# A two-block adaLN network on one core: k before q in the local layers, and small operations moved from GpSimd to VectorE

## The chip, the cores and the metric

The kernel runs on one core of a Trainium2 chip. The metric is the device time of one execution in microseconds (us); lower is better. Five engines work beside each other, each through its own queue in order: TensorE (PE in the profile, with its weight loads as PEld), VectorE (DVE), ScalarE (ACT), GpSimd (POOL) and SyncE (SP), which issues most of the DMAs.

## The reference

The input is x, 4 sequences of 1024 tokens with 128 features, all in float32. Two adaLN blocks follow each other. Each computes six modulation vectors from a condition c, and then

```
h = layernorm(x) * (1 + ca) + sa;  x = x + ga * attention(h)
h = layernorm(x) * (1 + cb) + sb;  x = x + gb * ffn(h)
```

Block 0 has a linear attention (softmax over features, 16 heads) and a mixture of 16 small experts. Block 1 has a causal window attention (window 64, 16 heads of 8, a global prefix of 16 tokens), and its "ffn" is two local layers. A local layer, which is where most of the change lies, is

```
h = shift_token(x)                                   # half of the features from the token before
q, k, v = split(h @ wqkv)                            # 8 heads of 64
q = q / max(|q|, 1e-12) * q_scale ; k = k / max(|k|, 1e-12) * k_scale
q, k = rotary_xpos(q, k)
o = softmax(8 * q k^T over this and the previous window of 64, masked) v
x = x + o @ wo
h = layernorm(shift_token(x)) * g + b ;  a, g = split(h @ w1 + b1) ; x = x + (a * gelu(g)) @ w2 + b2
```

The layernorm is (x - mean) / sqrt(var + 1e-5).

## The kernel before

The work is tiled by 128 tokens. Features lie on partitions (`xT`, `hT`), so that matmuls contract over them; layernorms and norms of heads are computed with tokens on partitions. The program has four stretches in time: block 0's attention (to about 75 us), the experts with the next sequences' attention woven in (to about 320 us), block 1's window attention (to about 579 us) and the local layers (to the end), 2 layers x 4 sequences x 8 tiles = 64 tiles.

PE's order is written out by hand (`manual_schedule`); the orders of DVE, ACT and POOL come from a scheduler that places each instruction by its own estimate of times. Its result for both kernels can be read from the built programs, and the prediction uses it.

`ln_in` (L133) is every layernorm's first half. DVE takes the statistics (`bn_stats`, `bn_aggr`, L144 and L146), subtracts the mean (L150); POOL adds 1e-5 to the variance (L152), raises it to the power -1/2 (L153) and multiplies (L154). `ln_out` transposes the result on PE and applies scale and bias on ACT. There are 49 such calls.

`project(l, b, t, w, ps)` (L647) makes q (w=0) or k (w=1) of one tile. PE multiplies (L653) into a bank of PSUM. ACT squares it (L656, `sq`). DVE multiplies it by the rotary cosine table (`co`, L658) and, with halves exchanged, by the sine table (`si`, L663), and sums the squares of each head (L665) into column w of `ss`, a tile of 128 x 2 x 8. POOL then, for w=1, takes the maximum of both columns with 1e-24 (L668), raises both to -1/2 (L669), adds `co` and `si` (L673, for q too), and multiplies k by its column (L675). q is not multiplied; its column enters the scores as a scale.

In the first eight tiles (`light`, layer 0, sequence 0, t >= 3) q's `si` isn't added on POOL: PE adds both while it transposes them (L849).

In the local layers' loop, step g of PE holds: the scores of tile g (`scores`, L875, 32 matmuls at L885), the two projections of tile g+2, the transposes of the weights of tile g-2 (`flip`, L926), the transposes of q and k of tile g+1 (`turn`, L845), the outputs of tile g-3, the values, and a share of the MLP. ACT copies the transposed q (L852), DVE the transposed k (`kT`, L858). DVE reads the scores with mask and q's scale (L892, eight per tile, each takes a maximum too), ACT exponentiates (L904), and `over_sums` divides by the sums: POOL and DVE take one half of the heads each (both L919; the sums' reciprocal is L912). In the `light` tiles ACT takes DVE's half. The MLP of 512 tokens is spread over four tiles: `mlp_in` (a layernorm), `mlp_gate`, `mlp_up` (`ge`, L997 on DVE), `mlp_down` (L1004).

The order of PE around the change:

```
            when(g, scores)
            when(g + 2, project_mid, 0)
            ...
            when(g - 2, flip, 0)
            when(g - 1, over_sums)
            when(g + 2, project_mid, 1)
            when(g - 2, flip, 1)
            when(g, exps)
```

The first three tiles' projections are made in the stretch before (L821).

Of the kernel before, what the change touches and what calls it, by code (L numbers as in the profile page):

```python
# [22 lines left out]
ALU = mybir.AluOpType  # L23
# [3 lines left out]
P = 128  # L27
# [9 lines left out]
HEADS, DH, DEPTH = 8, 64, 2  # L37
# [11 lines left out]
def adaln_blocks(ctx: ExitStack, tc: tile.TileContext, a: dict, out: bass.AP):  # L49
    nc = tc.nc  # L50
    pe, act, dve, pool = nc.tensor, nc.scalar, nc.vector, nc.gpsimd
# [4 lines left out]
    def const(name, shape, dtype=F32):  # L56
        return cp.tile(shape, dtype, tag=name, name=name)
# [5 lines left out]
    def bc(ap, shape):  # L63

        return ap.unsqueeze(len(ap.shape)).to_broadcast(shape)
# [39 lines left out]
    nhalf = const("nhalf", [P, 4])  # L105
# [27 lines left out]
    def ln_in(tp, src, wp, name, bufs=None, n=4):  # L133

        if src is not None:
            for i in range(4):
                pe.transpose(tp[:, i, :], src[:, i * P : (i + 1) * P], ident)
        tps = tp if isinstance(tp, list) else [tp]
        h, w = len(tps), D // len(tps)
        st = wp.tile([P, 4, 2, 6], F32, tag="st", name=f"st_{name}")  # L140
        mv = wp.tile([P, 4, 2], F32, tag="mv", name=f"mv_{name}")
        for i in range(n):
            for e in range(h):
                dve.bn_stats(st[:, i, e, :], tps[e][:, i, :])  # L144
        for i in range(n):
            dve.bn_aggr(mv[:, i, :], st[:, i, 0:h])  # L146

        xh = wp.tile([P, 4, D], F32, tag="xh", name=f"xh_{name}", bufs=bufs)
        for e in range(h):
            dve.tensor_tensor(xh[:, 0:n, e * w : (e + 1) * w], tps[e][:, 0:n], mv[:, 0:n, 0:1].to_broadcast([P, n, w]), ALU.subtract)  # L150
        rv = wp.tile([P, 4, 1], F32, tag="rv", name=f"rv_{name}")
        pool.tensor_scalar(rv[:, 0:n], mv[:, 0:n, 1:2], 1e-5, None, ALU.add)  # L152
        pool.tensor_tensor(rv[:, 0:n], rv[:, 0:n], nhalf[:, 0:n].unsqueeze(2), ALU.pow)  # L153
        ln_in.last = pool.tensor_tensor(xh[:, 0:n], xh[:, 0:n], rv[:, 0:n].to_broadcast([P, n, D]), ALU.mult)  # L154
        return xh
# [53 lines left out]
    NG8 = B * NT  # L209
# [390 lines left out]
    def const1(name, shape):  # L600
        return c1.tile(shape, F32, tag=name, name=name)

    wl = []
    for l in range(DEPTH):
        w = [const1(f"wqkv_{l}", [P, 3, HEADS * DH]), const1(f"wo_{l}", [P, 4, D]), const1(f"w1_{l}", [P, 2 * HID]), const1(f"w2_{l}", [P, 3, D])]
# [38 lines left out]
    late = {}  # L644
    pj = ctx.enter_context(tc.tile_pool(name="pj", bufs=3))

    def project(l, b, t, w, ps):  # L647


        nt = f"{l}_{b}_{t}_{w}"  # L650
        if w == 0:
            late[l, b, t, "ss"] = pj.tile([P, 2, HEADS], F32, tag="ss", name=f"ss_{nt}", bufs=4)
        pe.matmul(ps, lhsT=hs[l, b][:, t * P : (t + 1) * P], rhs=wl[l][0][:, w, :], start=True, stop=True)  # L653
        ph = ps.rearrange("p (h e) -> p h e", e=DH)
        sq = pj.tile([P, HEADS, DH], F32, tag="sq", name=f"sq_{nt}", bufs=2)
        act.activation(sq, ph, AF.Square)  # L656
        co = pj.tile([P, HEADS, DH], F32, tag=f"co{w}", name=f"co_{nt}")
        dve.tensor_tensor(co, ph, abs_[l][:, 0, t, w, :].unsqueeze(1).to_broadcast([P, HEADS, DH]), ALU.mult)  # L658
        si = pj.tile([P, HEADS, DH], F32, tag="si", name=f"si_{nt}", bufs=3)

        ex = bass.AP(tensor=ps.tensor, offset=ps.offset + 32, ap=[ps.ap[0], [DH, HEADS], [-32, 2], [1, 32]])
        sn = abs_[l][:, 1, t, w, :].rearrange("p (i e) -> p i e", i=2).unsqueeze(1).to_broadcast([P, HEADS, 2, 32])
        dve.tensor_tensor(si.rearrange("p h (i e) -> p h i e", i=2), ex, sn, ALU.mult)  # L663
        ss = late[l, b, t, "ss"]
        dve.tensor_reduce(ss[:, w, :], sq, AX.X, ALU.add)  # L665
        if w == 1:

            pool.tensor_scalar(ss, ss, 1.0e-24, None, ALU.max)  # L668
            pool.tensor_tensor(ss, ss, nhalf[:, 0:2].unsqueeze(2).to_broadcast([P, 2, HEADS]), ALU.pow)  # L669
        if w == 0 and light(l, b, t):  # L670
            late[l, b, t, "si"] = si
        else:
            pool.tensor_tensor(co, co, si, ALU.add)  # L673
        if w == 1:
            pool.tensor_tensor(co, co, bc(ss[:, 1, :], [P, HEADS, DH]), ALU.mult)  # L675
        late[l, b, t, "co", w] = co

    def light(l, b, t):

        return (l, b) == (0, 0) and t >= EARLY  # L680
# [5 lines left out]
    with (  # L686
# [28 lines left out]
        def weights(b, t):  # L715

            sv, mx = kept1[b, t, "s"]
            for j in range(4):
                if (b, t) != (0, 0):
                    maximum(b, t, j)  # L720
                mj = mx[:, 4 * j : 4 * j + 4]
                pr = kept1[b, t, "pr", j] = wp.tile([P, 4, KV], F32, tag="pr", name=f"pr_{b}_{t}_{j}", bufs=8)
                if j < 3:
                    dve.tensor_tensor(pr, sv[j], bc(mj, [P, 4, KV]), ALU.add)
                    act.activation(pr, pr, AF.Exp)
                else:
                    for h in range(4):
                        act.activation(pr[:, h, :], sv[j][:, h, :], AF.Exp, bias=mj[:, h : h + 1])
# [61 lines left out]
        def when(g, f, *args):  # L790
            if 0 <= g < NG8:
                f(*divmod(g, NT), *args)

        for g in range(-1, NG8 + 2):
            b, t = divmod(g, NT)
            ahead = 0 <= b and b + 1 < B
            if g == -1:
                weights(0, 0)
            when(g + 2, scores)
            when(g + 2, weights)  # L800
            if ahead and t in (2, 4):
                queries(b + 1, t // 2 - 1)
            for after, k, f in ((6, 0, tokens), (8, 0, normed), (11, 1, tokens), (13, 1, normed)):
                if (g - after) % NT == 0 and 0 <= (g - after) // NT < B - 1:
                    f((g - after) // NT, k, "h3")
            for at, k, f in ((1, 0, tokens), (3, 0, normed), (5, 1, tokens), (7, 1, normed)):
                if g == at:
                    f(B - 1, k, "h2")
            when(g - 1, back)
            when(g + 1, flip, (0, 1))  # L810
            when(g + 1, values)
            when(g, outputs)
            when(g + 1, flip, (2, 3))
            if t == 5 and 0 < b <= DEPTH:
                rotary(tab, abs_[b - 1], b - 1)
            if g % 4 == 1 and g > 4:
                project_out((g - 5) // NT, (g - 5) % NT // 4)
            if ahead and t in (3, 5):
                keys(b + 1, t // 2 - 1)

            for i, w in ((0, 0), (0, 1), (1, 0), (1, 1), (2, 0), (2, 1))[max(0, g - NG8 + 6) : max(0, g - NG8 + 7)]:  # L821
                project(0, 0, i, w, ps.tile([P, BLK], F32, tag="t", name=f"qk_0_0_{i}_{w}", bufs=2))

    both.close()
# [4 lines left out]
    with (  # L829
# [198 lines left out]
        for l in range(DEPTH):  # L1028
            for b in range(B):
                g = (l * B + b) * NT  # L1030
# [29 lines left out]
        def project_mid(l, b, t, w):  # L1060
            if (l, b) != (0, 0) or t >= EARLY:
                project(l, b, t, w, pM.tile([P, BLK], F32, tag="mid", name=f"qk_{l}_{b}_{t}_{w}"))

        for g in range(-1, tiles + 4):
            side = steps.get(g, [])
            when(g, scores)
            when(g + 2, project_mid, 0)

            turns = {-1: (0, 1), 0: (2,), 1: ()}.get(g, (g + 1,))
            if 1 < g < NT - 1:  # L1070
                when(g + 1, turn, 0)
            when(g - 2, flip, 0)
            when(g - 1, over_sums)
            when(g + 2, project_mid, 1)
            when(g - 2, flip, 1)
            when(g, exps)
            for i in turns:
                if not 1 < g < NT - 1:
                    when(i, turn, 0)
                if i < EARLY and g < EARLY:  # L1080
                    when(i, turn, 1)
            when(g - 3, outputs)
            if g >= EARLY - 1:
                when(g + 1, turn, 1)
            for f, args in side[:1]:
                f(*args)

            for i in {0: (), 1: (0,)}.get(g, (g - 1,)):
                when(i, values)

            f0 = g - 7
            if f0 % 4 == 0 and 0 <= f0 < tiles - NT:
                lo = f0 % NT * P
                project_out(f0 // (B * NT), f0 // NT % B, lo, lo + BLK)
            for f, args in side[1:]:
                f(*args)
# [127 lines left out]
```

## Time and profile before

| what | value |
|---|---|
| median of 3 runs | 1243.0 us (1241.72 to 1243.09) |
| profiled execution, its own time | 1246.33 us |
| its span | 1244.5 us |
| mean granted clock of TensorE | 0.983 |
| busy: PE, DVE, ACT, POOL | 1162.8, 878.8, 817.8, 823.3 us |
| bytes moved by DMA | 51.04 MB |

The span is what the profile shows from the first to the last instruction of one execution; its own time, 1.8 us longer, holds what lies around it. Busy time is the sum of an engine's instructions. A line of a group gives line, engine, operation, tiles and shapes, how often, and then busy time in us and the mean of one in ns, and the idle time just before them. A line of the order in time gives start in us, duration in us, engine, line and operation, and in brackets how long the engine was idle before and what ended that.

### The profile page before, as it was taken

The page shows a single profiled execution, that of the slowest core. Times are in us where ns is not written, and L with a number is a line of the kernel's source. Part 1 is how long each engine was busy: PE and PEld are TensorE (multiplying, and loading weights), DVE is VectorE, ACT ScalarE, POOL GpSimd, SP SyncE. Part 2 cuts the span into 40 slices and gives each one's busy share as a digit, 9 for nine tenths or more (in the row PEclk, how much of TensorE's full clock was granted, in tenths as well). Part 3 has the DMA queues.
Part 4 walks back from the last instruction along what each step waited for, and adds up shares of the span by engine and source line. Part 5 has one row for each costly group of instructions (what it writes and reads, how often), then busy time and mean ns, then how long its engine had stood idle before and what let it go on. Part 6 is the DMA issues. An engine that isn't in the chain of part 4 may idle for free.

```text
span 1244.5 us, 34772 instructions
## 1 busy us (share of the span) xinstructions
PE 1162.8 (93%) x13578; PEld 714.7 (57%) x13578; DVE 878.8 (71%) x2798; ACT 817.8 (66%) x2223; POOL 823.3 (66%) x813
## 2 busy tenths in 40 slices
PE   6789999999899999988898999999999999999998
PEld 5644453534476667755665556665555556565564
DVE  5556263452476667666878988898898888998864
ACT  3363373322577677766886788788877887788862
POOL 4436445746334445444889988888899889888840
PEclk8699999999999999999999999999999999999999
DMA  6040404021400000000112111111111111111110
GB/s 179 1 130 8 138 0 132 7 74 63 137 4 4 3 20 14 11 3 3 35 27 48 27 35 26 32 40 27 39 28 34 39 29 45 38 27 31 36 40 26
DMA packets 36136, 51.04 MB, mean 41 GB/s; under 512 B 5850, under 2 KB 17668, under 8 KB 35844
## 3 DMA queue, kind: packets, MB, share of 16 engines
q1 hardware_dynamic: 35540, 48.29, 14.1%
q8 instruction: 107, 1.75, 0.6%
q10 hardware_dynamic: 432, 0.53, 0.1%
q14 instruction: 57, 0.47, 0.1%
HBM read 26.52 MB, written 2.36 MB: 23 GB/s over the span
## 4 chain that ended last, share of the span: by engine, by line
PE 43%; DVE 27%; ACT 18%; POOL 7%; issue 5%; DMA 1%; POOLq 0%; ACTq 0%; SPq 0%; DVEq 0%
ACT pr L904 5%; PE h L489 4%; PE yp L951 4%; DVE pr L892 3%; DVE co L658 3%; PE s L885 3%; DVE si L663 3%; DVE ss L665 3%; PE ptr L735 3%; PE qk L653 3%; POOL u L494 2%; ACT sq L656 2%; PE s L261 2%; PE obank L752 2%; DVE ge L997 2%
## 5 line engine op out<-in xcount | busy, mean ns | idle before, releaser
L904 ACT ACTIVATE pr<-pr,mx 128x128 f32<-128x128 f32 x512 | 200.8, 403 | 88.2 <-DVE mx L892 88.1
L673 POOL TENSOR_TENSOR co<-co,si 128x512 f32<-128x512 f32 x123 | 156.7, 1280 | 79.5 <-DVE si L663 72.2
L669 POOL TENSOR_TENSOR ss<-ss,nhalf 128x16 f32<-128x16 f32 x64 | 191.7, 2995 | 5.3
L892 DVE CUSTOM_DVE_ANT_0 pr<-s,masks,ss 128x128 f32<-128x128 f32 x512 | 144.2, 342 | 42.4 <-PE s L885 42.0
L653 PE MATMUL qk<-wqkv,hs 128*128 128x512 f32 x256 | 137.7, 620 | 4.9 <-ACT pt L737 4.9
L494 POOL TENSOR_TENSOR u<-u,cw 128x512 f32<-128x512 f32 x64 | 81.1, 1271 | 74.4 <-ACT u L492 74.4
L489 PE MATMUL h<-hT,w 128*128 128x512 f32 x256 | 123.8, 605 | 4.0 <-DVE g L496 4.0
L496 DVE TENSOR_TENSOR g<-u,h 128x512 f32<-128x512 f32 x64 | 43.8, 686 | 114.9 <-POOL u L494 114.9
L279 DVE TENSOR_REDUCE mx<-s 128x4 f32<-128x448 f32 x128 | 73.5, 617 | 56.4 <-PE s L270 56.4
L658 DVE TENSOR_TENSOR co<-qk,ab 128x512 f32<-128x512 f32 x128 | 86.7, 677 | 26.0 <-ACT sq L656 26.0
L904 ACT ACTIVATION_READ_ACCUMULATOR pr<-pr,mx 128x1 f32 x512 | 101.7, 199 | 0.0
L492 ACT ACTIVATE u<-h 128x512 f32<-128x512 f32 x64 | 38.2, 598 | 93.2 <-PE h L489 85.7
L926 PEld LDWEIGHTS ptr<-ident,pr 128*128 128x128 f32 x512 | 63.5, 141 | 61.6 <-issue 54.8
L663 DVE TENSOR_TENSOR si<-qk,ab 128x512 f32<-128x512 f32 x128 | 86.8, 678 | 0.0
L489 PEld LDWEIGHTS h<-hT,w 128*128 128x128 f32 x256 | 48.3, 194 | 66.2 <-issue 51.0
L665 DVE TENSOR_REDUCE ss<-sq 128x8 f32<-128x512 f32 x128 | 86.2, 673 | 0.0
L656 ACT ACTIVATE sq<-qk 128x512 f32<-128x512 f32 x128 | 74.9, 586 | 14.8 <-PE qk L653 12.3
L845 PE MATMUL qktr<-ident,co 128*128 128x128 f32 x492 | 76.9, 280 | 6.6 <-POOL co L675 5.3
L885 PEld LDWEIGHTS s<-kT,qT 64*64 64x64 f32 x2048 | 56.8, 134 | 45.6 <-issue 22.1
L919 POOL TENSOR_TENSOR pr<-pr,sm 128x512 f32<-128x512 f32 x64 | 74.7, 1168 | 7.9 <-DVE sm L912 7.9
L885 PE MATMUL s<-kT,qT 64*64 64x128 f32 x2048 | 72.1, 277 | 7.6 <-DVE kT L858 6.1
L737 ACT COPY pt<-ptr 112x512 f32<-112x512 f32 x128 | 72.5, 612 | 8.6 <-PE ptr L735 8.6
(212 smaller groups left out, 2871.2 us busy)
## 6 DMA issues: line engine op xcount, KB each, us to landing
cw<-cd SPq DMA_DIRECT2D x128, 128.0 KB, 3.0
ve<-vs SPq DMA_DIRECT2D x120, 128.0 KB, 2.3
hs<-hT SPq DMA_DIRECT2D x16, 256.0 KB, 3.2
out<-out SPq DMA_DIRECT2D x7, 256.0 KB, 2.7
xin<-in_x SPq DMA_DIRECT2D x3, 512.0 KB, 6.1
w<-in_w SPq DMA_DIRECT2D x3, 512.0 KB, 5.0
wqkv<-in_wqkv SPq DMA_DIRECT2D x2, 768.0 KB, 5.3
ab<-in_tab SPq DMA_DIRECT2D x1, 1024.0 KB, 7.3
```

The lines of the kernel that those rows point to most:

```text
L489: pe.matmul(h, lhsT=w[:, c * P : (c + 1) * P], rhs=hT[b][:, blk(k)], start=True, stop=True)
L494: pool.tensor_tensor(u, u, kept[b, k, "cw"][:, c, :], ALU.mult)
L653: pe.matmul(ps, lhsT=hs[l, b][:, t * P : (t + 1) * P], rhs=wl[l][0][:, w, :], start=True, stop=True)
L656: act.activation(sq, ph, AF.Square)
L658: dve.tensor_tensor(co, ph, abs_[l][:, 0, t, w, :].unsqueeze(1).to_broadcast([P, HEADS, DH]), ALU.mult)
L663: dve.tensor_tensor(si.rearrange("p h (i e) -> p h i e", i=2), ex, sn, ALU.mult)
L665: dve.tensor_reduce(ss[:, w, :], sq, AX.X, ALU.add)
L669: pool.tensor_tensor(ss, ss, nhalf[:, 0:2].unsqueeze(2).to_broadcast([P, 2, HEADS]), ALU.pow)
L673: pool.tensor_tensor(co, co, si, ALU.add)
L885: pe.matmul(S[j][qs, c, :], lhsT=q[rw, c, qs], rhs=k[rw, c, at : at + P], start=True, stop=True)
L892: dve.tensor_tensor_reduce(out=pr[:, c, :], in0=S[j][:, c, :], in1=mk[:, min(t, 1), :], scale=kept[l, b, t, "ss"][:, 0, h : h + 1], scalar ...
L904: act.activation(pr[:, c, :], pr[:, c, :], AF.Exp, bias=mx[:, j, c : c + 1], scale=-1.0, accum_out=sm[:, j, c : c + 1])
```

## The change

k is projected before q, in the stretch before and in the loop. `ss` is made by whichever comes first. Each of the two maxima is taken by itself, 128x8, on DVE, right after the sum in the program's text. The power is taken in two parts of 128x8 on POOL: k's before k's multiplication, q's after q's addition. In every layernorm the addition of 1e-5 is on DVE instead of POOL. PE's other steps stay where they were.

```diff
-        pool.tensor_scalar(rv[:, 0:n], mv[:, 0:n, 1:2], 1e-5, None, ALU.add)
+        dve.tensor_scalar(rv[:, 0:n], mv[:, 0:n, 1:2], 1e-5, None, ALU.add)
...
-        if w == 0:
+        if (l, b, t, "ss") not in late:
             late[l, b, t, "ss"] = pj.tile([P, 2, HEADS], F32, tag="ss", name=f"ss_{nt}", bufs=4)
...
         dve.tensor_reduce(ss[:, w, :], sq, AX.X, ALU.add)
+        dve.tensor_scalar(ss[:, w], ss[:, w], 1.0e-24, None, ALU.max)
         if w == 1:
-
-            pool.tensor_scalar(ss, ss, 1.0e-24, None, ALU.max)
-            pool.tensor_tensor(ss, ss, nhalf[:, 0:2].unsqueeze(2).to_broadcast([P, 2, HEADS]), ALU.pow)
+            pool.tensor_tensor(ss[:, 1], ss[:, 1], nhalf[:, 0:1].to_broadcast([P, HEADS]), ALU.pow)
         if w == 0 and light(l, b, t):
             late[l, b, t, "si"] = si
         else:
             pool.tensor_tensor(co, co, si, ALU.add)
         if w == 1:
             pool.tensor_tensor(co, co, bc(ss[:, 1, :], [P, HEADS, DH]), ALU.mult)
+        else:
+            pool.tensor_tensor(ss[:, 0], ss[:, 0], nhalf[:, 0:1].to_broadcast([P, HEADS]), ALU.pow)
...
-            for i, w in ((0, 0), (0, 1), (1, 0), (1, 1), (2, 0), (2, 1))[max(0, g - NG8 + 6) : max(0, g - NG8 + 7)]:
+            for i, w in ((0, 1), (0, 0), (1, 1), (1, 0), (2, 1), (2, 0))[max(0, g - NG8 + 6) : max(0, g - NG8 + 7)]:
...
-            when(g + 2, project_mid, 0)
+            when(g + 2, project_mid, 1)
...
-            when(g + 2, project_mid, 1)
+            when(g + 2, project_mid, 0)
```

## The prediction

> **What bounds the kernel now.** I read the page's busy shares and slices first, then busy time by stretch, then who waits for whom on PE, then the groups by line, and last the order in time on DVE and POOL.
>
> ```profile
> PE 1162.8 (93%) x13578; PEld 714.7 (57%) x13578; DVE 878.8 (71%) x2798; ACT 817.8 (66%) x2223; POOL 823.3 (66%) x813
> ...
> PE   6789999999899999988898999999999999999998
> ...
> POOL 4436445746334445444889988888899889888840
> ```
>
> PE is full from slice 20 (about 620 us) on, and POOL is at 8 to 9 tenths there. By stretch (columns: PE, PEld, DVE, ACT, POOL busy us, then granted clock):
>
> ```profile
> 640.00:700.00 60.00, 55.46 (x593) 35.09 (x590) 50.80 (x179) 47.56 (x157) 55.38 (x47) 1.00 0.15 35
> ...
> 880.00:940.00 60.00, 59.72 (x572) 35.89 (x571) 49.82 (x170) 48.20 (x145) 51.94 (x41) 1.00 0.15 34
> ```
>
> Between 720 and 1180 PE idles under 1 us in 60; nothing can be won there except those last tenths, and much can be lost. Around 640 to 700 POOL is full and PE idles 4.5 us. PE's waits, first in 579 to 760, then in 760 to 1180 (total us, times, longest):
>
> ```profile
> PE qktr L845 <- POOL co L675: 5.3, 3, 3.0
> PE s L885 <- DVE kT L858: 3.5, 6, 1.8
> ```
>
> ```profile
> PE s L885 <- DVE kT L858: 2.6, 10, 0.3
> ```
>
> So what the change aims at, PE waiting for k's multiplication on POOL, is 5.3 us in three waits, all early. What is left later is a wait of 0.22 to 0.30 us for the copy of kT by DVE, once in four tiles: at 754, 794, 834, 873.72 and so on to 1154, eleven times, every 40 us. It is at zero slack: in that place DVE has been busy without a gap since 858.22 and stays so until 882.6.
>
> **The change part by part.** First POOL. Its rows:
>
> ```profile
> L669 POOL TENSOR_TENSOR ss<-ss,nhalf 128x16 f32<-128x16 f32 x64 | 191.7, 2995 | 5.3
> L153 POOL TENSOR_TENSOR rv_h<-rv_h,nhalf 128x4 f32<-128x4 f32 x32 | 34.7, 1086 | 2.4
> L668 POOL TENSOR_SCALAR ss<-ss 128x16 f32<-128x16 f32 x64 | 25.4, 397 | 1.3
> ```
>
> A power of 16 columns takes 2.92 us undisturbed, of 4 columns 1.04. The 8-column power is not in the trace; it lies between these two, and on the line through them it is 1.04 + 4 x 0.157 = 1.67. Two of them are 3.34 against 2.92 + 0.26 (the maximum that leaves): POOL's work per tile changes by +0.16 us by quiet times, by 0 by mean times (2 x 1.70 against 2.995 + 0.397). 49 additions of about 0.23 us leave POOL. POOL is no faster per tile; only k comes out earlier, since max, half of the power and the place after q go: 0.34 + 1.25 + about 1.8 (second place on DVE, 849.79 against 847.99) = 3.4 us earlier. q comes out later, after k: add 1.27, power 1.67 and multiplication 1.04 pass ahead of its addition. By the times laid out below its addition then ends at about 865.3 and PE transposes it at 867.73: 2.4 us in hand, so it costs nothing there. The waits of PE for k at 597.95 (3.00), 583.97 (1.00) and 677.08 (1.25) should go: **-5.2 us**. Projection, transposes and scores keep their number on PE; w=0 and w=1 only change places, and no DMA is moved.
>
> Then DVE, which gets 128 maxima (128x8) and 49 additions (128x4). Alone each is cheap: TENSOR_SCALAR rows of 128x4 take 0.16 us and start 0.07 to 0.1 apart. But look at DVE beside POOL:
>
> ```profile
> 252.08 0.81 DVE L431 TENSOR_SCALAR rank_g<-rank_g 128x32 f32<-128x32 f32 x1
> ...
> 921.32 1.42 DVE L919 TENSOR_TENSOR pr<-pr,sm 128x512 f32<-128x512 f32 x1
> ...
> 834.55 0.72 DVE L919 TENSOR_TENSOR pr<-pr,sm 128x512 f32<-128x512 f32 x1
> ```
>
> ```profile
> 251.51 1.34 POOL L494 TENSOR_TENSOR u<-u,cw 128x512 f32<-128x512 f32 x1 [1.31 <-ACT u L492]
> ...
> 919.69 2.50 POOL L673 TENSOR_TENSOR co<-co,si 128x512 f32<-128x512 f32 x2
> ...
> 834.50 2.93 POOL L669 TENSOR_TENSOR ss<-ss,nhalf 128x16 f32<-128x16 f32 x1
> ```
>
> L431, the same kind of instruction as the new maximum, takes 0.17 us when POOL is idle; here it ends at 252.89, as POOL's 512-column instruction ends at 252.85. The same at 179.58 (0.92) and, for a 128x4 one, L125 at 9.96 (1.02, under POOL's L154). L919 at 921.32 is stretched to 1.42 by L673, and at 834.55, beside a power, not at all. So a small DVE instruction from SBUF to SBUF waits out a running 512-column POOL instruction, but not a power.
>
> The Trainium skill ("SBUF — State Buffer", Who interferes with whom) says this of the port pair that VectorE and GpSimd share: tensor_scalar can take both ports, and whoever is second waits for the whole instruction. It speaks against this change. The row at 834.55 differs from it, as the power held nobody back; by the rule each power could hold one more DVE instruction for up to 1.67 us, some 11 x 1.67 = 18 us more.
>
> Now lay the new order on DVE over the traced times of the tile with zero slack. The built order there is: co, si, sum (k), co (q), maximum, si, sum (q), kT, maximum, three ge, bn, s, xh, addition, seven s; next tile: co, si, sum (k), reciprocal, maximum, co (q), L919, si, sum, kT. Starts on DVE lie 0.60 apart for 512 columns. First tile: k's si ends at 859.51, POOL's addition runs 859.65 to 860.92, the maximum is due at 860.62, so +0.35. kT is then at 862.16 and q's maximum due at 862.75; k's power ends on POOL at 862.7 and its multiplication wants to start at 862.8: the maximum gets in (+0.1) or waits 1.0 (+1.1). The addition falls beside q's power: +0.1. Next tile: si ends near 870.4, POOL adds until 871.75, the maximum is due at 871.05: +0.8. In POOL's built order its pr (L919, 1.04) comes next, until 872.9, and DVE's own L919, due at 872.45, waits 0.4 (0.1 of it today). The sum is 0.35 + 0.1 + 0.1 + 0.8 + 0.3 = **1.7 us** on kT, and PE, waiting already, takes all of it; 2.7 if the multiplication gets in first, and 0.4 if nothing waits (four instructions at 0.1). I take 1.7, since the four rows above show the wait. In the other two tiles of four the same waits (two maxima of k at 0.35, two of q at 0.1 to 1.1, two L919 at up to 0.7: 2.3 to 4.3 us) fall into DVE's gaps of 2.1, 1.9, 0.8 and twice 0.5 us: nothing. Eleven such places and the one near 670, where DVE is full too: 12 x 1.7 = **+20 us**. If that cover in the other tiles were gone, up to 2 us more per group.
>
> Layernorms: the addition now stands behind the subtraction on DVE. At 46.98 to 48.1 it also stands behind a reciprocal, so the power starts 1.1 us later; PE waits for that product at 49.81 (2.15 us today), and the start is one chain: +1 (between -0.9, since POOL's subtraction at 18.84 comes forward by 1, and +2). In the tail three layernorms are waited for (gm for hn, 1.9 us): 0.5 each, **+1.5**. Between 75 and 320 an addition can wait for L494 (1.27), but PE's gaps there are few: -1 to +2, taken as 0.
>
> The sum: -5.2 + 20 + 1 + 1.5 = +17.5 us. The profiled execution took 1246.33 us for a span of 1244.5, 3.3 above the median of 1243.0; the differences are added to the median: 1260.5 us.
>
> **The rivals.** *Faster, 1238 us.* If a maximum of 8 columns slips past POOL, each new DVE instruction costs only its 0.07: four a group, 12 x 0.28 = 3.4. Against it stand -5.2, -0.9 at the start, and -2 if k's earlier place also gives back half of the 4.5 us that PE idles in 640 to 700: -4.7. It decides at 0.1 us for a maximum. For it: half of today's L919 are undisturbed (median 0.725, mean 0.808). Against: they fall beside the power, and the new order puts DVE's small instructions beside the additions.
> *About as before, 1244 us.* Nothing waits, but 0.4 x 12 = 4.8 and the layernorms' 2.5 eat the 5.2: +2.
> *POOL as the bound.* From 632 to 697 POOL is full; +0.16 a tile and 0.2 for a power that waits on DVE's maximum give 7 x 0.36 = +2.5 in place of the -1.25 there; without the waits on DVE that is -4 + 2.5 + 2.5 (layernorms) + 3.4 = +4.4, 1247. Elsewhere POOL idles 1.3 us or more per tile.
> *More than forecast.* With 2.7 a group and 2 lost in the early stages: 33 + 5 - 3 = +35 to +40, 1280.
>
> **How the numbers follow.** The lock at 1 to 2.7 us a group: 0.68 (of it 0.15 above 2.2). About as before: 0.12, of which 0.08 within 0.2% and 0.04 above it. POOL as the bound: 0.06. Faster: 0.14. A measurement of this kernel tells 0.2%, 2.5 us, from no change. Slower 0.78, same 0.08, faster 0.14. The range runs from 1242, which leaves out most of the faster case, to 1283, 2.75 x 12 and the small terms.
>
> **What would show it.** The maximum's group on DVE at 0.4 to 0.8 us mean instead of 0.16; L919 on DVE above 0.81; PE waiting for kT L858 some 20 us in place of 6.1; PE <- POOL co L675 near zero; POOL's 128x8 power at 1.6 to 1.75. If the maximum's mean is under 0.2, or PE waits for q's transpose instead, I am wrong.

## The result, and the profile after

The changed kernel takes 1278.35 us (median of 6 runs, 1274.93 to 1283.83) against 1243.05 us for the kernel before on the same chip: ratio 1.0281, 95% interval 1.0253 to 1.0308. That is 35 us slower, where 17.5 were forecast. The sign and the mechanism of the main term were right; the sum was half of what came, and one of its terms, the gain of 5.2 us for k's waits, went the other way.

The busy times and one stretch of the changed kernel, to set beside those of before (stretch: PE, PEld, DVE, ACT, POOL busy us, granted clock, DMA):

```profile
PE 1170.4 (92%) x13578; PEld 712.8 (56%) x13578; DVE 953.5 (75%) x2975; ACT 817.6 (64%) x2223; POOL 814.0 (64%) x764
```

```profile
880.00:940.00 60.00, 56.35 (x525) 32.75 (x524) 54.32 (x177) 41.54 (x132) 52.29 (x41) 1.00 0.14 34
```

DVE has 75 us more work, POOL 9 us less. From 880 to 940 PE now idles 3.7 us in 60 in place of 0.3, and DVE is at 54.3 of 60. Who waits for whom on PE, in 579 to 760 and then in 760 to 1160 (total us, times, longest):

```profile
PE s L886 <- DVE kT L859: 10.5, 7, 3.9
```

```profile
PE s L886 <- DVE kT L859: 12.1, 9, 1.4
PE yp L952 <- DVE si L663: 3.7, 10, 0.4
```

PE's wait for k's multiplication on POOL is gone from the list. Its wait for DVE's copy of k went from 0.3 us to as much as 1.4 us each time. The groups on DVE in the local layers: DVE's half of the division by the sums before (L919), then the same after (L920) and the new maximum (L666):

```profile
L919 DVE TENSOR_TENSOR pr<-pr,sm 128x512 f32<-128x512 f32 x59 | 47.7, 808 | 1.3
```

```profile
L920 DVE TENSOR_TENSOR pr<-pr,sm 128x512 f32<-128x512 f32 x58 | 62.7, 1082 | 1.3
L666 DVE TENSOR_SCALAR ss<-ss 128x8 f32<-128x8 f32 x122 | 54.8, 450 | 0.1
```

The maximum has a mean of 0.45 us where the forecast's condition for the waits was 0.4 to 0.8, and L920 rose from 0.81 to 1.08. Of all 128 maxima, 85 take over 0.2 us (53.6 us together), and each of these 85 ends within 0.04 us of the end of one of POOL's 512-column instructions. In the rows below, DVE first and then POOL, the first maximum ends at 880.18, POOL's addition at 880.15; the second at 884.35, k's multiplication at 884.32; the third lies wholly inside a power and takes 0.15, as do all eight that lie so (0.15 to 0.16):

```profile
879.37 0.81 DVE L666 TENSOR_SCALAR ss<-ss 128x8 f32<-128x8 f32 x1
...
883.41 0.94 DVE L666 TENSOR_SCALAR ss<-ss 128x8 f32<-128x8 f32 x1
...
902.95 0.15 DVE L666 TENSOR_SCALAR ss<-ss 128x8 f32<-128x8 f32 x1
```

```profile
878.88 1.27 POOL L672 TENSOR_TENSOR co<-co,si 128x512 f32<-128x512 f32 x1 [1.03 <-PE qktr L846]
...
883.28 1.04 POOL L674 TENSOR_TENSOR co<-co,ss 128x512 f32<-128x512 f32 x1
...
901.78 1.65 POOL L668 TENSOR_TENSOR ss<-ss,nhalf 128x8 f32<-128x8 f32 x1
```

In the two profiled executions the start differs too: the first copy of kT is at 580.4 us before and at 572.8 after. Over all kernels below it lies between 572 and 584, with the layernorms' addition on either engine, so this is spread between executions. The local layers are therefore compared by the time between the first and the last copy of kT in each trace: 608.9 us before, 645.4 after, +36.5, close to the 35.3 of the medians. Each such time comes from one execution.

### The profile page after: what moved, and what is told of

It reads as the page before. It is cut to its first block, busy times and chain, and to the rows that moved or that the text cites. A ratio compares the mean times of both kernels' runs of the same rounds, so it can differ in the third digit from the quotient of the medians.

```text
span 1273.3 us, 34764 instructions
## 1 busy us (share of the span) xinstructions
PE 1170.4 (92%) x13578; PEld 712.8 (56%) x13578; DVE 953.5 (75%) x2975; ACT 817.6 (64%) x2223; POOL 814.0 (64%) x764
## 3 DMA queue, kind: packets, MB, share of 16 engines
q1 hardware_dynamic: 35540, 48.29, 13.6%
## 4 chain that ended last, share of the span: by engine, by line
DVE 37%; PE 36%; ACT 16%; issue 5%; POOL 4%; DMA 1%; POOLq 0%; SPq 0%; ACTq 0%; DVEq 0%
DVE pr L893 6%; PE yp L952 5%; PE h L489 4%; DVE co L658 4%; DVE si L663 4%; DVE ss L665 4%; ACT pr L905 4%; DVE ss L666 3%; PE s L886 3%; PE ptr L736 3%; PE s L261 2%; POOL u L494 2%; DVE ge L998 2%; PE y L504 2%; PE obank L753 2%
## 5 line engine op out<-in xcount | busy, mean ns | idle before, releaser
L672 POOL TENSOR_TENSOR co<-co,si 128x512 f32<-128x512 f32 x123 | 164.8, 1340 | 110.1 <-DVE si L663 95.8
L668 POOL TENSOR_TENSOR ss<-ss,nhalf 128x8 f32<-128x8 f32 x64 | 111.6, 1743 | 6.0 <-DVE ss L666 0.7
L676 POOL TENSOR_TENSOR ss<-ss,nhalf 128x8 f32<-128x8 f32 x64 | 111.0, 1734 | 1.7 <-DVE ss L666 1.1
```

What stands on the lines that cost most here:

```text
L668: pool.tensor_tensor(ss[:, 1], ss[:, 1], nhalf[:, 0:1].to_broadcast([P, HEADS]), ALU.pow)
L676: pool.tensor_tensor(ss[:, 0], ss[:, 0], nhalf[:, 0:1].to_broadcast([P, HEADS]), ALU.pow)
```

## The experiments

Each was timed in five rounds beside the kernel before on its own chip. "Local" is the time from the first to the last copy of kT in the profiled execution; "mid" is the time of four tiles between 760 and 1030 us, "late" the mean time of four tiles over 16 tiles near the end (from the 46th to the 62nd copy of kT).

| kernel | median us | ratio to before (95%) | local | mid | late |
|---|---|---|---|---|---|
| before | 1243.05 | 1 | 608.9 | 39.8 | 40.35 |
| after | 1278.35 | 1.0281 (1.0253 to 1.0308) | 645.4 | 42.05 | 43.1 |
| max_on_pool | 1247.57 | 1.0019 (0.9999 to 1.0039) | 616.1 | 39.9 | 41.5 |
| max_as_reduce | 1259.56 | 1.0120 (1.0097 to 1.0143) | 627.0 | 40.6 | 42.75 |
| max_as_tt | 1280.27 | 1.0301 (1.0276 to 1.0325) | 646.2 | 42.05 | 43.1 |
| max_twice | 1288.36 | 1.0349 (1.0325 to 1.0374) | 654.7 | 42.65 | 43.6 |
| ln_on_pool | 1282.06 | 1.0287 (1.0262 to 1.0312) | 641.7 | 42.0 | 43.15 |
| k_max_dve | 1272.01 | 1.0220 (1.0186 to 1.0254) | 639.3 | 41.95 | 43.0 |
| q_max_dve | 1249.17 | 1.0026 (1.0005 to 1.0046) | 616.5 | 40.0 | 41.55 |
| sum_first | 1272.47 | 1.0232 (1.0204 to 1.0260) | 640.0 | 41.95 | 42.35 |
| order_only | 1251.03 | 1.0056 (1.0038 to 1.0073) | 616.0 | 39.85 | 41.4 |
| before_max_dve | 1270.77 | 1.0213 (1.0182 to 1.0245) | 632.8 | 41.45 | 42.25 |
| before_ln_dve | 1241.53 | 0.9993 (0.9972 to 1.0014) | 611.5 | 40.1 | 40.7 |
| fold_ln | 1249.76 | 1.0044 (1.0025 to 1.0063) | 619.6 | 40.3 | 41.3 |
| before_fold | 1246.13 | 1.0027 (1.0011 to 1.0042) | 609.9 | 39.8 | 40.4 |
| split_fold | 1253.14 | 1.0086 (1.0067 to 1.0106) | 617.1 | 40.35 | 41.4 |

The theory is the one on record: a small instruction on DVE from SBUF to SBUF waits out POOL's running 512-column instruction ("the lock"). The rivals: any further instruction on DVE costs this much since its stretch before kT has no slack; the new order and the two powers cost it; the layernorms cost it.

**The maxima back on POOL (max_on_pool).** The edit:

```
-        dve.tensor_scalar(ss[:, w], ss[:, w], 1.0e-24, None, ALU.max)
         if w == 1:
+            pool.tensor_scalar(ss[:, 1], ss[:, 1], 1.0e-24, None, ALU.max)
...
         else:
+            pool.tensor_scalar(ss[:, 0], ss[:, 0], 1.0e-24, None, ALU.max)
```

> The changed kernel with the maxima back on GpSimd, each (128x8) just ahead of its power; k first and the layernorms' addition on VectorE stay. If VectorE's maxima cost the time, by the wait or by their number: 1243 to 1252 (GpSimd has 2 x 0.25 us more per tile and 1.3 us or more of idle time for it, so nothing to 5 us is lost there). If k first with two powers costs it: 1268 to 1280.

1247.57 us, ratio 1.0019: 2.6% of the 2.8% goes with DVE's maxima. The new order isn't the cause of the bulk.

**The same maximum as a reduction (max_as_reduce).** The edit:

```
-        dve.tensor_reduce(ss[:, w, :], sq, AX.X, ALU.add)
-        dve.tensor_scalar(ss[:, w], ss[:, w], 1.0e-24, None, ALU.max)
+        s2 = pairs[w][t % 4]                       # 128x8x2, odd places hold 1e-24
+        dve.tensor_reduce(s2[:, :, 0], sq, AX.X, ALU.add)
+        dve.tensor_reduce(ss[:, w, :], s2, AX.X, ALU.max)
```

> The changed kernel with the maximum written as a reduction: the sums go to the even places of a 128x8x2 tile whose odd places hold 1e-24, and a TENSOR_REDUCE (max) over the pairs gives what the TENSOR_SCALAR gave. Same engine, same place, same order on VectorE and TensorE, one instruction for one. If the cost is that a TENSOR_SCALAR from SBUF to SBUF waits out GpSimd's running instruction (the theory on record): the 512-column reduction just ahead of it is never stretched in the traces (0.67 us in all 122), so the short one takes under 0.2 us each in place of 0.45, four tiles take 39.8 to 40.4 us in place of 42.05, and the time falls by 22 to 30 us to 1248 to 1256. If any further instruction on VectorE costs that much because its stretch before the k copy has no slack: no change, 1278 (within 4). If the new order or the two powers cost it: no change, 1278.

1259.56 us: 1.6% of the 2.6% went with the form of the instruction alone, on the same engine, in the same place. The new group and L925, the same half of the division, in the local layers:

```profile
L925 DVE TENSOR_TENSOR pr<-pr,sm 128x512 f32<-128x512 f32 x59 | 60.6, 1028 | 1.3
...
L671 DVE TENSOR_REDUCE ss<-pair 128x8 f32<-128x16 f32 x122 | 19.6, 161 | 0.1
```

No reduction takes over 0.173 us. The forecast of 1248 to 1256 was missed by 4 us: L925 is still stretched (1.03 us against 0.85 in max_on_pool). Mid-way this is the whole rest: behind a copy of kT that PE waits for, L925 at 877.49 takes 1.50 us beside k's multiplication (877.40 to 878.44), where its counterpart in max_on_pool takes 0.81; DVE has no gap in that tile, and four tiles take 0.7 us more than in max_on_pool. A wait not paid by the maximum is partly paid by the next instruction that can be held.

**The same maximum with two operands in SBUF (max_as_tt).** The edit:

```
-        dve.tensor_scalar(ss[:, w], ss[:, w], 1.0e-24, None, ALU.max)
+        dve.tensor_tensor(ss[:, w], ss[:, w], floor, ALU.max)      # floor: 128x8 of 1e-24
```

> The changed kernel with the maximum as a TENSOR_TENSOR against a 128x8 tile that holds 1e-24: same engine, place and order, one instruction for one, but two operands read from SBUF. L920, also a TENSOR_TENSOR with both operands in SBUF, is stretched beside GpSimd's 512-column instructions (up to 1.6 us), the reduction with one never was. If two SBUF operands are enough to wait: mean 0.35 to 0.5 us and 1270 to 1282. If only the TENSOR_SCALAR form waits: under 0.2 us and 1256 to 1263, as the reduction.

1280.27 us, and the new group waits like the TENSOR_SCALAR:

```profile
L669 DVE TENSOR_TENSOR ss<-ss,floor 128x8 f32<-128x8 f32 x122 | 51.2, 419 | 0.1
```

The Trainium skill ("SBUF — State Buffer", Who interferes with whom) says that a tensor_tensor with both inputs in SBUF contends with GpSimd's reads and that a tensor_reduce on trn2 never does. The two runs agree: 0.42 against 0.16 us in the same place.

**The maximum twice (max_twice).** Every L666 line is followed by a copy of itself.

> The changed kernel with every maximum issued twice in a row on VectorE (the second changes nothing). If the cost is waiting out GpSimd's running instruction: the first has waited already and GpSimd's next is mostly a power, which holds nobody back, so most of the second ones take 0.15 us; four to six more in the stretch without slack at 0.07 us each, and a second wait of up to 1 us where GpSimd goes straight to another 512-column instruction (about a quarter of the 128 cases in the trace): 1281 to 1293. If each instruction costs the same wherever it stands (0.45 us mean): 128 more cost as much as the first 128, 1300 to 1312.

1288.36 us, 0.7% above the changed kernel's ratio, in the range of the waiting theory and well below that of a price per instruction. The two groups:

```profile
L666 DVE TENSOR_SCALAR ss<-ss 128x8 f32<-128x8 f32 x123 | 57.8, 470 | 0.1
...
L921 DVE TENSOR_TENSOR pr<-pr,sm 128x512 f32<-128x512 f32 x59 | 42.4, 718 | 0.3
...
L667 DVE TENSOR_SCALAR ss<-ss 128x8 f32<-128x8 f32 x123 | 34.3, 279 | 0.2
```

The first still pays 0.47; half of the second ones take under 0.172 us. And L921 fell to 0.72, so the second maximum partly pays what L920 paid.

**The layernorms' addition back on POOL (ln_on_pool), and alone on DVE (before_ln_dve).** The edit is `dve.tensor_scalar(rv...)` to `pool.tensor_scalar(rv...)` in the changed kernel, and the reverse in the kernel before.

> The changed kernel with the layernorms' addition back on GpSimd; all else stays. The trace of the changed kernel reaches the local layers about 9 us earlier than that of before, with GpSimd's addition no longer behind the 512-column products of the expert stage: if that is a gain of the addition on VectorE, this one loses 3 to 9 us, 1281 to 1287. By the prediction's term (+1 at the start, +1.5 in the tail, 0 in between) it gains 2.5 us, 1275.5. If the addition is the main cost, 1250 to 1265.

> The kernel before with only the layernorms' addition moved to VectorE. By the runs with the maxima on GpSimd (layernorms' addition on VectorE 1.0019, on GpSimd 1.0056): a gain of 2 to 5 us, 1238 to 1242. By the pair with the maxima on VectorE (1.0281 and 1.0287): nothing, 1242 to 1245. By the prediction's term: 1245.5.

Ratios 1.0287 against 1.0281, and 0.9993 with an interval that holds 1: in these two pairs the addition is worth nothing that can be told. A third pair, max_on_pool (1.0019) and order_only (1.0056, below), differs by this addition too; its intervals just touch, so a gain of some us there is neither shown nor excluded. The gain of 3 to 9 us expected of it, read from the early start of one trace, was spread between executions.

**The order alone (order_only).** k first, two powers of 8, all else on POOL as before.

> Only the order of the change: k projected ahead of q, two powers of 8 columns; maxima (128x8 each) and the layernorms' addition on GpSimd as before. By the run with the maxima on GpSimd (0.2% over the kernel before) and that with the layernorms' addition on GpSimd (0.1% over the changed kernel): 1246 to 1252. By the prediction's term for k's waits (-5.2 us) and GpSimd's longer work (2 x 0.25 in place of 0.4): 1238 to 1243.

1251.03 us, 0.56% slower, in the first range. PE's waits from 570 to 705 show why the -5.2 us did not come:

```profile
PE s L887 <- DVE kT L860: 6.8, 6, 3.4
PE qktr L847 <- POOL co L672: 2.6, 1, 2.6
```

Before, PE waited 3.00 us for k's multiplication at 597.95 and 1.25 at 677.08. Now it waits 3.38 at 594.67 for DVE, which copies kT only after the next tile's work, and 2.61 at 670.74 for q's addition on POOL, which stands behind k's power and multiplication. Mid-way the order costs nothing (39.85), but four of the late tiles take 1.05 us more. Nearly all of this lies in one tile of four, in which DVE has no idle time from one copy of kT to the next: 8.41 us before (from 1072.45), 9.42 in order_only (from 1070.76). Two of DVE's own instructions are held there: `xT` takes 0.93 us in place of 0.75, and DVE's half of the division 1.53 in place of 0.70, as it now meets k's multiplication where a power ran before. DVE before, DVE and POOL in order_only:

```profile
1074.49 0.70 DVE L919 TENSOR_TENSOR pr<-pr,sm 128x512 f32<-128x512 f32 x1
```

```profile
1072.98 1.53 DVE L921 TENSOR_TENSOR pr<-pr,sm 128x512 f32<-128x512 f32 x1
```

```profile
1072.47 1.49 POOL L674 TENSOR_TENSOR co<-co,ss 128x512 f32<-128x512 f32 x1
```

So the order's late loss is the same lock, without any new instruction on DVE.

**The maxima alone (before_max_dve).** The kernel before with two dve maxima in place of POOL's one of 128x16.

> The kernel before with only the maximum moved to VectorE, as two of 128x8: q first, one power of 16 columns, the layernorms' addition on GpSimd. If VectorE's maxima cost it in any order, since each follows its sum while GpSimd adds the same projection's co and si: 1262 to 1278, the maxima's mean at 0.3 to 0.5 us. If only the new order lines them up with GpSimd's additions: 1244 to 1252, mean under 0.2.

1270.77 us, mean 0.42 us: the wait does not need the new order. In both orders the maximum follows its sum while POOL adds the same projection's `co` and `si`.

**The maximum ahead of `si` (sum_first).** The edit moves two lines and holds their order:

```
+        dve.tensor_reduce(ss[:, w, :], sq, AX.X, ALU.add)
+        here(dve.tensor_scalar(ss[:, w], ss[:, w], 1.0e-24, None, ALU.max))
         ...
+        here(dve.tensor_tensor(si..., ex, sn, ALU.mult))
-        dve.tensor_reduce(ss[:, w, :], sq, AX.X, ALU.add)
-        dve.tensor_scalar(ss[:, w], ss[:, w], 1.0e-24, None, ALU.max)
```

> The changed kernel with the sum of squares and its maximum moved ahead of si, and the maximum held ahead of si on VectorE: GpSimd's addition of co and si can't run yet then. As many instructions as the changed kernel. If the larger part of the loss is waiting out GpSimd's running 512-column addition: k's maxima take 0.15 to 0.25 us each, q's 0.15 to 0.6 (they can still meet k's multiplication), and the time falls by 8 to 20 us of the 19 that the reduction form won, to 1258 to 1270. If a maximum costs the same wherever it stands: 1274 to 1282.

1272.47 us, outside both ranges. Of 128 maxima 101 now take under 0.2 us (mean 0.32). But q's maximum right behind the copy of kT that PE waits for still takes 1.04 to 1.05 us, above the 0.6 expected: it waits out POOL's addition for k, once in four tiles. DVE, then POOL:

```profile
879.68 1.05 DVE L662 TENSOR_SCALAR ss<-ss 128x8 f32<-128x8 f32 x1
```

```profile
879.43 1.26 POOL L673 TENSOR_TENSOR co<-co,si 128x512 f32<-128x512 f32 x1
```

PE waits for something else from 760 to 1160:

```profile
PE qktr L847 <- POOL co L673: 8.2, 9, 0.9
PE s L887 <- DVE kT L860: 2.8, 9, 0.3
```

q's maximum and kT now stand ahead of q's `si`, so a held maximum makes q's addition on POOL late, 0.9 us once in four tiles. The wait for kT is at its old 0.3. The same lock reaches PE by another path; the run agrees with the theory and is no gain.

**Which of the two maxima (k_max_dve, q_max_dve).** In each, one of the two stays on DVE and the other stands on POOL ahead of its power.

> The changed kernel with q's maximum back on GpSimd ahead of q's power; k's stays on VectorE. In the changed kernel's trace k's maxima hold up the gap-free stretch 866.75 to 894.3 by 0.24 + 0.73 + 0.18 = 1.15 us per four tiles, q's by 0.07 + 0.85 + 0.07 = 1.0. If both tiles of that stretch reach the end, k's alone is about half of the loss: 1257 to 1264, four tiles take 41.0 us. If only the waits ahead of the copy of k count, as the prediction laid it out, k's is nearly all: 1266 to 1276.

> The changed kernel with k's maximum back on GpSimd ahead of k's power; q's stays on VectorE. If both tiles of the gap-free stretch reach the end, q's alone is the other half: 1256 to 1264, four tiles take 40.9 us. If the gaps of the second tile cover its wait, as the prediction had it, 0.2 us per four tiles are left: 1248 to 1252.

k's alone gives 1.0220, q's alone 1.0026 (max_on_pool: 1.0019). Against max_on_pool k's is 2.0 and q's 0.1 of the 2.6%; the other 0.5% shows only with both, and by the time between the copies of kT nearly all of it (5.3 of 6.1 us) lies in the first 20 tiles. Mid-way k's is nearly all of it (41.95 against 42.05), as the prediction had laid it out, and the later reading, half each, was wrong. How q's 0.85 us in the changed trace can count for nothing is seen in k_max_dve, DVE first, then POOL:

```profile
880.84 1.80 DVE L922 TENSOR_TENSOR pr<-pr,sm 128x512 f32<-128x512 f32 x1
```

```profile
879.82 1.04 POOL L675 TENSOR_TENSOR co<-co,ss 128x512 f32<-128x512 f32 x1
880.83 1.26 POOL L673 TENSOR_TENSOR co<-co,si 128x512 f32<-128x512 f32 x1
```

Without q's maximum in front of it, L922 at 880.84 waits out k's multiplication and q's addition itself: 1.80 us where it takes 0.69 undisturbed. The wait belongs to POOL's instructions, and whichever DVE instruction of the kind comes next pays it. With k's maximum on POOL too (max_on_pool) the same instruction, at 871.0, takes 0.81. That k's maximum had shifted POOL and DVE so that the two meet is the likely reason; it was not tried by itself.

**No maximum at all (fold_ln, before_fold, split_fold).** The squares get a 65th column per head that holds 1e-24, so the sum is sum + 1e-24. fold_ln is the changed kernel with this, before_fold the kernel before, and split_fold is before_fold with k's power of 8 ahead of its multiplication and q's behind it.

```
+        sq = sqs[len(late_n) % 2]                  # 128x8x65, last column 1e-24
+        act.activation(sq[:, :, 0:DH], ph, AF.Square)
...
-            pool.tensor_tensor(ss, ss, ..., ALU.pow)
+            pool.tensor_tensor(ss[:, 1], ss[:, 1], ..., ALU.pow)      # split_fold
             pool.tensor_tensor(co, co, bc(ss[:, 1, :], [P, HEADS, DH]), ALU.mult)
+            pool.tensor_tensor(ss[:, 0], ss[:, 0], ..., ALU.pow)      # split_fold
```

> The changed kernel without a maximum instruction on any engine: the squares are kept with a 65th column per head that holds 1e-24, and the one reduction that sums them adds it (sum + 1e-24 in place of the maximum of the two). The layernorms' addition stays on VectorE. If the maxima are all that the change loses by: 1238 to 1246, no L920 stretched beyond the 0.81 to 0.85 mean of the kernels without VectorE's maxima. If VectorE's stretch before the k copy is late for another reason too: 1250 to 1260.

> The kernel before with the 65th column of 1e-24 in place of the maximum (sum + 1e-24); order, one power of 16 and the layernorms as before. GpSimd has one instruction fewer per tile (0.40 us mean), so k's multiplication is 0.34 us earlier: the three waits of the tensor engine for it (3.0, 1.25, 1.0) shrink by about 1 us: 1241.5 to 1243.5. If the reduction over 65 columns costs VectorE 0.01 us each on the path: 1244 to 1246.

> As before_fold, and the power split: 8 columns for k ahead of its multiplication, 8 for q behind it; q is still projected and added first, and VectorE's and the tensor engine's orders are those of the kernel before. k's multiplication is 1.25 + 0.34 = 1.6 us earlier without q becoming later: the waits of 3.0, 1.25 and 1.0 become 1.4, 0 and 0, -3.9 us: 1238 to 1241. If, as in the run with the order alone, the wait for VectorE's copy of k (kT) takes their place: 1243 to 1245.

1249.76, 1246.13 and 1253.14 us: all three above the kernel before, and above the range that each was given first. split_fold was expected to gain 3.9 us and loses 10.7 against the kernel before (0.86%). Against before_fold, from which it differs only by the split of POOL's power, with DVE's and PE's orders unchanged, it is 7.0 us slower. Its L924, and the same line in before_fold:

```profile
L924 DVE TENSOR_TENSOR pr<-pr,sm 128x512 f32<-128x512 f32 x59 | 75.5, 1280 | 1.3
```

```profile
L923 DVE TENSOR_TENSOR pr<-pr,sm 128x512 f32<-128x512 f32 x59 | 44.6, 756 | 1.3
```

With the split, DVE's half of the division starts just after POOL has begun to add `co` and `si` and waits out nearly all of it (from 874.36, 1.69 us, the addition from 874.23 to 875.49); in before_fold 24 of the 59 lie inside a power and take 0.71. The mean grows by 0.52 us. None of these runs beats the kernel before by more than the noise.

## Why the prediction was wrong, step by step

Two terms failed. The -5.2 us assumed that q's addition has time in hand and that nothing else is late where k's waits go; the runs show a loss in its place. The +20 us for the maxima had the right mechanism and was too small; 29 came. The time between the first and the last copy of kT takes the +36.5 us apart, with max_on_pool and order_only for the order and the rest for the maxima.

- **-5.2 us for k's waits: wrong, a loss of up to 7 in its place.** The waits for k's multiplication did go. What the prediction did not ask is what comes late next where a wait goes: DVE's copy of kT (3.38 us) and q's addition (2.61) did. By stretches, order_only against before: +2.8 in the first 20 tiles, 0 mid-way, +4.2 late, where DVE's division is held. "2.4 us in hand" for q was true of the one group that was laid out, not of the early and late ones. This step is 12 of the missing 18 us by these traces. By the medians of whole kernels the order costs 7.0 us in order_only but only 2.4 in max_on_pool, so the share is 8 to 12.
- **+20 us, 12 groups at 1.7: right in kind and place, too low, +29.** Against max_on_pool the changed kernel loses 13.6 us in 27 tiles mid-way, 2.0 per four against 1.7. The laid-out waits up to kT came to 0.24 + 0.07 + 0.07 + 0.73 + 0.32 = 1.43 in the trace (after), for 1.65 put down. The rest lies behind that kT, in the next tile, where L920 or q's maximum waits 0.9 us: the tile that ends with that kT takes 12.2 us against 11.2 in max_on_pool, the next 9.1 against 8.0, the other two the same within 0.15. The prediction itself said that DVE has no gap there until 882.6, and its sum still stopped at 872.9.
- **The early groups: counted as one at 1.7, the first 20 tiles cost 10.3 us** (the last 17 another 5.4). Up to 4.8 of the 10.3 us go with the granted clock. The stretches 580 to 610, 640 to 670 and 670 to 700 of the changed kernel, then of max_on_pool (the number after POOL's count is the clock):

```profile
580.00:610.00 30.00, 25.06 (x225) 17.39 (x224) 26.74 (x94) 22.05 (x82) 20.72 (x17) 0.89 0.12 28
...
640.00:670.00 30.00, 23.89 (x301) 16.05 (x303) 28.04 (x104) 19.82 (x70) 27.12 (x22) 0.96 0.22 50
670.00:700.00 30.00, 29.95 (x263) 18.01 (x258) 25.80 (x83) 23.75 (x71) 23.29 (x19) 0.93 0.08 19
```

```profile
580.00:610.00 30.00, 25.83 (x243) 17.70 (x236) 26.04 (x94) 23.05 (x86) 23.54 (x23) 0.94 0.12 28
...
640.00:670.00 30.00, 26.32 (x315) 17.04 (x314) 27.74 (x110) 21.28 (x73) 27.76 (x28) 1.00 0.22 50
670.00:700.00 30.00, 28.77 (x287) 17.34 (x286) 23.41 (x77) 24.27 (x74) 29.19 (x29) 1.00 0.08 19
```

  At 30 us each, 0.11 + 0.04 + 0.07 below full clock is 6.6 us of clock, against 0.06 and 1.8 us; how much of that reached the end is an estimate. PE's waits for kT are 3.92 us at 593.55 and 3.76 at 668.64, against 3.38 and 2.37 in max_on_pool; in k_max_dve (3.92 and 2.87) the clock is 0.94 in the first stretch and 1.00 in the other two. The Trainium skill ("TensorE: Matmul & The Clock Gate", HAM oscillation — how this bites in real kernels) gives the rule of no PE-idle gaps over about 3.4 us. As a threshold these traces don't bear it out. In order_only a wait of 3.38 us (594.67) leaves the clock at 1.00, and one of 2.61 us (670.74) is followed by 0.94; in the kernel before, 0.94 comes with a wait of 3.00 us (597.95). The stretches 580 to 610 and 670 to 700 of order_only:

```profile
580.00:610.00 30.00, 25.57 (x268) 17.40 (x262) 27.00 (x95) 24.36 (x89) 25.14 (x25) 1.00 0.12 28
...
670.00:700.00 30.00, 29.16 (x270) 18.08 (x274) 21.15 (x61) 22.28 (x65) 27.62 (x28) 0.94 0.08 19
```

  What sets the clock is left open: no run changed the length of a wait alone.
- **+2.5 us for the layernorms: wrong, nothing.** before_ln_dve measures 0.9993.
- **The signs to look for.** The maximum at 0.45 us, L920 at 1.08, PE waiting 24 us for kT in place of 6.1 (10.5, 12.1 and 1.3 later on), POOL's power of 8 at 1.74: all as named. "PE <- POOL co near zero" holds too, and says less than was thought, since the wait had only moved.
- **The chances.** "The lock" carried 0.68, and its upper part, more than forecast at 1280, is what came; that it did is in part luck, since it came by the order's loss and the early tiles, and not by 2.7 a group. "POOL as the bound" did not come: POOL's work fell, and q came late through its place in the queue.

The reading that the prediction weighed and left, by which every power holds a DVE instruction back, would have added 18 us and come out at the measured time, for a wrong reason: the eight maxima that lie wholly inside a power take 0.15 to 0.16 us.

## What to carry to other kernels

Before a small operation is moved from GpSimd to VectorE, look at what GpSimd runs at the moment the operation will start: from SBUF to SBUF its price was the rest of a 512-column addition or multiplication (0.45 us on average here, 0.15 undisturbed), though not of a power. Of the three forms tried only the reduction was free of it. Lay out the whole stretch without a gap, not only up to the first instruction that somebody waits for, and where a stall goes, read in the same tile who is second. When a wait is paid by one instruction, taking that instruction away may only hand it to the next: price GpSimd's instruction, not VectorE's.

## What the runs showed of the hardware that was not expected

- The wait is mutual. POOL's power at 881.11 of the changed kernel takes 2.10 us in place of 1.64; DVE's L920 runs until 881.70.
- The form decides: in one place and order, a 128x8 maximum takes 0.45 us as TENSOR_SCALAR, 0.42 as TENSOR_TENSOR with two SBUF operands, 0.16 as TENSOR_REDUCE. The Trainium skill ("SBUF — State Buffer", Who interferes with whom) has the shared pair held for the whole instruction by whoever issues first; the 85 long maxima agree for POOL's 512-column instructions, and the eight inside powers (0.15 to 0.16 us) do not.
- Splitting one POOL instruction, with DVE's order untouched, moved 31 us of busy time onto DVE (59 times 0.52) and 7 us onto the end (split_fold against before_fold).
